# Two graph-attention layers, 16 batches: row sums of three groups counted in two parts, bias added by GpSimd, small transfers at other steps

## The chip, the cores and the metric

The kernel runs on one core of one Trainium2 chip. The metric is the device time of one execution in microseconds (us). The engines are called here as the profile calls them: PE (TensorE, matrix products; PEld is its weight load), DVE (VectorE), ACT (ScalarE), POOL (GpSimd) and SP (SyncE, which here only issues transfers).

## The reference

Sixteen graphs of 1024 nodes with 256 features go through two layers. Each is a layer norm, a relu, a masked multi-head attention and a residual sum. Layer 0 has 4 heads of 64, layer 1 has 8 heads of 32 and biases on its projections.

```python
# layer 0
h = relu(layernorm(x))
x = x + attention(h, adj > 0, heads=4) @ Wo0.T + bo0
# layer 1
h = relu(layernorm(x))
x = x + attention(h, adj != 0, heads=8) @ Wo1.T + bo1
# attention, per head:
scores = q @ k.T / sqrt(D)
scores = where(mask, scores, -inf)
out = softmax(scores) @ v
```

## The kernel before

Everything is float32. For one batch, one layer and one half of the 512 query columns (`qh` 0 or 1) there are two **groups** (`g` 0 or 1). A group holds 128 feature rows: four heads of layer 1, or two heads of layer 0. It walks over the keys in **steps**, `j` = 0 to 7 in layer 1 and 0 to 3 in layer 0. A step works on one tile `p` of 128 x 4 x 512 numbers:

- `scores` (L448): four products on PE into two PSUM pairs `ps`. The pool of such pairs, `ps_s`, has three buffers, and the projections and `py` take theirs from it as well.
- `exponentials`: for each of the two pairs, DVE applies the mask and writes to `p` (L464), then ACT takes the exponential in place (L470).
- `weigh` (L482), two steps later (`LEAD = 2`): `p` times the values, summed over the steps in `po`.

The softmax sum over the keys needs the sum of all eight `p` of a group. In **layer 1** `count_steps` makes it. After each odd step, POOL adds the odd tile to the even one (L583, 128 x 2048 numbers), which leaves four tiles: (0,1), (2,3), (4,5), (6,7). Transfers issued by POOL with an addition at the target (`accumulate`, L569, 1 MB each) join them: (2,3) += (0,1) after step 3; (4,5) += (2,3) when step 7 comes up; (6,7) += (4,5) three steps later. Each waits, on POOL's own queue, until the one before has landed. Then `count` (L344) sums over the partitions on PE by four products with a column of ones, and adds up over its calls in PSUM `pz`. Even tiles have seven buffers (`p0`), odd ones two (`p1`). So the DVE operation of an odd step can write only when POOL has added the odd tile of four steps before. In **layer 0** `add_tiles` sums with DVE (L491, L494) and POOL (L494, L495, L497), without transfers.

When a group ends, `end_group` puts `spread` (ACT copies the sums out, SP sends them), `invert` (DVE), `fetch` (SP), `normalize` (POOL, L400) and, for the second group of a half, `end_half` (L430, L435) at fixed distances `at` from the step at hand.

**Order.** The whole program is one list of steps; `Stream.later(i, f)` puts a piece of work behind the instructions of step `i`, and `Stream.run` emits them. Nothing is reordered afterwards: each engine and each queue follows that written order. The work between is therefore a timetable. One **round** is 48 steps: `a` is the step at which layer 0 of batch b+1 begins (16 steps, round steps 0 to 15), `c` = `a` + 16 that at which layer 1 of batch b begins (round steps 16 to 47, four groups of eight). "Step 44" below is round step 44, the fifth step of the last group. A step that is followed by a projection or `py` (a "large" one) puts off its `weigh` to the next step.

Within a round the timetable also places, for batches ahead: the mask's load by POOL (`load`, L145), its transposition by SP (`flip`, L151) and its move to fp8 by ACT (`put`, L160); the statistics of a layer norm on DVE (L188 to L197, with L202 and L204 on POOL), the norm on ACT (L213); the addition of the output bias to `x` (`add_bias`, L222, a transfer with addition that POOL issues); `turn_blocks` on DVE (L239), then `put_blocks` and `place_blocks` (L244, L251), by which SP sends the transposed blocks to DRAM and back. The tile `adj` that a mask load fills has one buffer, so a load waits on POOL's queue until the flip of the one before has landed.

`gr.last` marks the fourth group of a layer, `gr.brief` that of batch 14, `gr.pairs` all groups of batch 15's layer 1; these have ways of their own.

Of the kernel before, what the change touches and what calls it, by code (L numbers as in the profile page):

```python
# [15 lines left out]
ALU = mybir.AluOpType  # L16
PSUM = bass.MemoryType.PSUM

P = 128
# [66 lines left out]
def fast_program(ctx, tc, a, w, loads, chk):  # L86
# [3 lines left out]
    nc = tc.nc  # L90
    x, adj, out = a["x"], a["adj"], a["out"]
    B, N, E = x.shape
    NT = N // P
# [42 lines left out]
    class Mask:  # L136
        def __init__(self, b):
            self.b, self.src, self.flipped, self.m = b, {}, {}, {}
# [32 lines left out]
    class Inputs:  # L171
# [47 lines left out]
        def add_bias(self, half):  # L219

            rows = xs[self.b, half]
            nc.gpsimd.dma_start(  # L222
                rows, w.bo[self.layer].unsqueeze(1).to_broadcast([P, 4, E]), accum_op=ALU.add
            )

        def blocks(self, half):
# [88 lines left out]
    class Group:  # L315


        def __init__(self, inp, mask, qh, g, half):
            self.inp, self.mask, self.qh, self.g, self.half = inp, mask, qh, g, half
            self.layer = inp.layer  # L320
            self.D = E // HEADS[self.layer]
            self.per = P // self.D
            self.scale = 1.0 / math.sqrt(self.D)
            self.n = f"{inp.n}_{qh}_{g}"
            self.n_f = self.per * 512 // P
            self.last = qh == QH - 1 and g == 1

            self.hurry = False

            self.brief, self.pairs = self.last and inp.b == B - 2, False  # L330

# [176 lines left out]
    class Stream:  # L508
# [12 lines left out]
        def later(self, i, f, *args):  # L521
            self.due.setdefault(i, []).append((f, args))
# [48 lines left out]
        def count_steps(self, i, st):  # L571


            gr, j = st.gr, st.j
            if gr.hurry and j >= NT - 2:
                if st.last:
                    self.counted(i, gr)
                gr.count(st.p, False, st.last)
            elif j % 2:
                one = self.steps[i - LEAD - 1].p  # L580
                if not (gr.brief or gr.pairs) and j == 7:
                    self.accumulate(gr.two, gr.one)
                nc.gpsimd.tensor_add(one, one, st.p)  # L583
                if gr.pairs:
                    self.later(i + 2, gr.count, one, j == 1, st.last)
                elif j == 1:
                    gr.one = one
                elif j == 3:
                    self.accumulate(one, gr.one)
                    gr.one = one  # L590
                    if gr.brief:
                        self.later(i + 8, gr.count, one, True, False)
                elif gr.brief:
                    self.later(i + (6 if j == 5 else 4), gr.count, one, False, st.last)
                elif j == 5:
                    gr.two = one
                else:
                    self.later(i + (1 if gr.last else 3), self.accumulate, one, gr.two)
                    self.later(i + (4 if gr.last else 8), gr.count, one, True, True)

        def counted(self, i, gr):

# [4 lines left out]
        def end_group(self, i, gr):  # L607

            if gr.hurry:
                for f in (gr.spread, gr.finish, gr.inp.test):  # L610
                    self.later(i, f)
                return

            if gr.layer == 0:
                self.later(i + 4, gr.count_added)
                at = 4, 6, 7, 9, 11
            else:
                at = (8, 12, 14, 17, 19) if gr.qh == 0 else (8, 11, 12, 14)
                if gr.pairs:
                    at = 2, 5, 6, 7, 9  # L620
                elif gr.last:
                    at = 4, 6, 7, 9, 11
            for k, f in zip(at, (gr.spread, gr.invert, gr.fetch, gr.normalize)):
                self.later(i + k, f)
            if gr.last:

                k = 7 if gr.layer or gr.inp.b == 0 else 37
                self.later(i + k if gr.inp.b + gr.layer < B - 1 else len(self.steps) + 2, gr.inp.test)
            if gr.g == 1:
                self.later(i + at[4], gr.end_half)  # L630
# [8 lines left out]
    mask, inp = masks[0], inputs[0][0]  # L639
# [73 lines left out]
    stream = Stream(steps)  # L713
    later = stream.later

    def norms(inp, half, *at, whole=False):

        for i, f in zip(at, (inp.stats, inp.stats, inp.norm, inp.norm)):
            rest = (whole,) if i in at[2:] else ()
            later(i, f, half, (0, 1) if i in (at[0], at[2]) else (2, 3), *rest)  # L720
        later(at[3] + 1, inp.add_bias, half)

    def half_inputs(inp, half, *at):

        for i, f in zip(at, (inp.turn, inp.k, inp.q, inp.values)):
            later(i, f, half)

    def block_inputs(inp, half, turn, place, *at):

        later(turn, inp.turn_blocks, half)  # L730
        later(place, inp.put_blocks, half)
        later(place + 1, inp.place_blocks, half)
        for i, f in zip(at, (inp.k, inp.q, inp.values)):
            later(i, f, half)

# [4 lines left out]
    for t in range(NT):  # L740
        i = 5 + 2 * t
        later(i - 3, masks[1].load, t)
        later(i - 2, masks[1].flip, t)
        later(i, masks[1].put, t)
    later(9, bias_of_v)
    norms(inputs[0][1], 0, 2, 3, 5, 6, whole=True)
    half_inputs(inputs[0][1], 0, 7, 8, 10, 12)
    norms(inputs[0][1], 1, 6, 7, 9, 10, whole=True)
    half_inputs(inputs[0][1], 1, 13, 14, 20, 16)
    for b in range(B - 1):  # L750
        mine, a, c = inputs[1][b], first[b + 1], second[b]
        if b == 0:

            norms(mine, 0, a + 5, a + 6, a + 8, a + 9, whole=True)
            half_inputs(mine, 0, a + 11, a + 12, a + 14, a + 14)
            norms(mine, 1, a + 13, a + 14, a + 15, c, whole=True)
            half_inputs(mine, 1, c + 1, c + 3, c + 6, c + 4)
        else:
            norms(mine, 0, a - 20, a - 19, a - 16, a - 15)
            block_inputs(mine, 0, a - 14, a - 12, a, a + 2, a + 8)  # L760
            norms(mine, 1, a - 14, a - 10, a - 8, a - 6)
            block_inputs(mine, 1, a, a + 6, c, c + 6, c + 2)
        for i, u in zip((0, 2, 4, 6, 8, 10, 12, 13), range(NT)):
            later(a + i, masks[b].second, u)
        if b + 2 < B:
            other, mask = inputs[0][b + 2], masks[b + 2]
            later(a + 5, open_x, b + 2, 0)
            later(a + 13, open_x, b + 2, 1)
            if b == 0:
                norms(other, 0, a + 14, a + 15, c + 2, c + 3)  # L770
                block_inputs(other, 0, c + 4, c + 5, c + 8, c + 16, c + 18)
                norms(other, 1, c + 3, c + 4, c + 6, c + 7)
                block_inputs(other, 1, c + 10, c + 11, c + 22, c + 26, c + 30)
            else:
                norms(other, 0, a + 10, a + 12, a + 13, a + 15)
                block_inputs(other, 0, c, c + 1, c + 8, c + 16, c + 18)
                norms(other, 1, c, c + 4, c + 5, c + 6)
                block_inputs(other, 1, c + 7, c + 8, c + 22, c + 26, c + 30)
            for i, t in zip((7, 12, 17, 22, 33, 37, 41, 45), range(NT)):
                later(a + i - 5, mask.load, t)  # L780
                later(a + i - 3, mask.flip, t)
                later(a + i, mask.put, t)
        else:
            last, e = inputs[1][b + 1], c + 32
            norms(last, 0, c + 5, c + 6, c + 8, c + 9)
            block_inputs(last, 0, c + 10, c + 11, c + 14, c + 16, c + 20)
            norms(last, 1, c + 13, c + 14, c + 16, c + 17)
            block_inputs(last, 1, c + 18, c + 19, c + 24, e + 6, e + 4)
            for u in range(NT):
                later(c + 8 + 2 * u, masks[b + 1].second, u)  # L790
    stream.run()
# [157 lines left out]
def kernel(  # L949
# [28 lines left out]
    with ExitStack() as fast, tc.manual_schedule():  # L978
        fast_program(fast, tc, a, w, loads, chk)
# [61 lines left out]
```

## Time and profile before

| | us |
|---|---|
| median of 3 runs | 3362.56 (3353.72 to 3362.99) |
| the profiled execution | 3362.77 |
| its span, first to last instruction | 3360.8 |
| one round in the middle (batch 4: layer 0 of batch 5 and layer 1 of batch 4) | 207.6 |

| engine | busy us | what it mostly does |
|---|---|---|
| PE | 3221.9 (96%) | L448 1214.2, L482 1013.4, L344 148.6 |
| DVE | 2514.4 (75%) | L464 1795.6, 1.214 each |
| ACT | 2254.8 (67%) | L470 1614.8, 1.056 each |
| POOL | 2317.3 (69%) | L583 1195.1, 4.689 each |

Every product of the program stands in the trace as two matmul records, so a step has 8 records on L448 and 8 on L482, a count in layer 1 has 8 on L344. Instructions of PE and DVE follow each other in order. Busy PE time holds time at a lower clock as well: the profile gives the granted clock beside it. A `p<-p` transfer takes 9.3 us from its issue to its landing (median of 178; 7.0 to 23.5), an `x<-bo` transfer 5.9 (64), a mask load 4.3 (128).

### The profile page before, as it was taken

How to read it: one execution, taken by the hardware profiler on the slowest of the kernel's cores; microseconds unless marked ns; L12 is line 12 of the kernel's file. 1: busy time of each engine (PE TensorE's matmuls, PEld its weight loads, DVE VectorE, ACT ScalarE, POOL GpSimd, SP SyncE). 2: the span in 40 equal slices, each digit the busy share in tenths (PEclk: the TensorE clock that was granted, in tenths of full speed). 3: DMA queues.
4: the chain of work that ended last, by engine and by line, in shares of the span. 5: the costliest groups of instructions: out<-in, count | busy, mean ns of one | idle time of the engine just before them, and what ended most of it. 6: DMA issues, size and time to landing. Idle time of an engine off the chain costs nothing.

```text
span 3360.8 us, 44052 instructions
## 1 busy us (share of the span) xinstructions
PE 3221.9 (96%) x16302; PEld 1225.2 (36%) x16302; DVE 2514.4 (75%) x2786; ACT 2254.8 (67%) x2472; POOL 2317.3 (69%) x1146
## 2 busy tenths in 40 slices
PE   8999998999999999999999999999999999999998
PEld 3433433334334333333333334333343333433332
DVE  5677785877868778687786868768687786877766
ACT  5666676676767666676676676766766676776765
POOL 3567576676766758677586776767767686685776
PEclk9999998999999999999999999999999999999999
DMA  7347569495684857758477584866839568493441
GB/s 144 61 82 154 119 137 139 93 168 117 137 156 99 162 111 143 152 106 163 107 152 139 116 159 103 156 123 132 157 92 168 114 140 152 97 172 78 104 89 31
DMA packets 388063, 421.93 MB, mean 126 GB/s; under 512 B 197760, under 2 KB 324992, under 8 KB 365056
## 3 DMA queue, kind: packets, MB, share of 16 engines
q0 software_dynamic: 77856, 253.78, 42.7%
q1 hardware_dynamic: 309984, 165.26, 21.2%
q8 instruction: 130, 2.13, 0.3%
q14 instruction: 93, 0.76, 0.1%
HBM read 149.95 MB, written 47.96 MB: 59 GB/s over the span
## 4 chain that ended last, share of the span: by engine, by line
PE 84%; DMA 6%; POOL 4%; DVE 3%; issue 1%; ACT 1%; SPq 0%; POOLq 0%; DVEq 0%; ACTq 0%
PE ps L448 30%; PE po L482 25%; PE pq L269 12%; PE py L430 7%; PE pv L305 7%; POOL p L583 4%; DMA adjT<-adj 3%; PE pz L344 3%; DVE p L464 2%; DMA p<-p 1%; ACT p L470 0%; ACT mask L160 0%; DMA vd<-vn 0%; DMA hT<-turned 0%; POOL p L569 0%
## 5 line engine op out<-in xcount | busy, mean ns | idle before, releaser
L464 DVE SCALAR_TENSOR_TENSOR p<-mask,ps 128x1024 f32<-128x1024 fp8e5 x1536 | 1795.6, 1214 | 621.4 <-PE ps L448 506.2
L470 ACT ACTIVATE p<-p 128x1024 f32<-128x1024 f32 x1536 | 1614.8, 1056 | 879.6 <-DVE p L464 835.4
L583 POOL TENSOR_TENSOR p<-p,p 128x2048 f32<-128x2048 f32 x255 | 1195.1, 4689 | 201.5 <-PE po L482 190.7
L448 PE MATMUL ps<-qT,kT 32*128 32x512 f32 (+1 forms) x6144 | 1214.2, 649 | 92.6 <-DVE p L464 90.5
L482 PE MATMUL po<-p,v 128*32 128x512 f32 (+1 forms) x6144 | 1013.4, 617 | 1.8 <-ACT cat L355 1.6
L448 PEld LDWEIGHTS ps<-qT,kT 32*128 32x128 f32 (+1 forms) x6144 | 383.6, 188 | 848.1 <-issue 376.1
L495 POOL TENSOR_TENSOR p<-p 128x1024 f32<-128x1024 f32 x128 | 302.4, 2363 | 316.5 <-DVE p L494 307.7
L482 PEld LDWEIGHTS po<-p,v 128*32 128x32 f32 (+1 forms) x6144 | 229.9, 119 | 708.6 <-issue 481.2
L494 POOL TENSOR_TENSOR p<-p 128x1024 f32<-128x1024 f32 x64 | 151.0, 2359 | 230.8 <-DVE vn L384 146.0
L269 PE MATMUL pq<-hT,wk 128*128 128x512 f32 x512 | 244.3, 621 | 14.4 <-DMA hT<-turned 5.7
L569 POOL DMA_DIRECT2D p<-p x178 | 177.8, 999 | 104.9 <-DMA p<-p 70.2
L269 PE MATMUL pq<-hT,wq 128*128 128x512 f32 x512 | 239.6, 611 | 0.0
L305 PE MATMUL pv<-wv,hT 128*128 128x256 f32 x1024 | 237.8, 385 | 0.0
L430 PE MATMUL py<-wo,cat 128*128 128x256 f32 x1008 | 233.5, 385 | 1.4
L305 PEld LDWEIGHTS pv<-wv,hT 128*128 128x128 f32 x1024 | 189.4, 190 | 71.3 <-issue 22.7
L430 PEld LDWEIGHTS py<-wo,cat 128*128 128x128 f32 x1008 | 186.6, 190 | 70.6 <-issue 43.0
L400 POOL TENSOR_TENSOR cat<-cat,inv 128x512 f32<-128x512 f32 x127 | 173.5, 1366 | 7.1 <-DMA inv<-vd 3.7
L160 ACT ACTIVATE mask<-adjT,numbers 128x1024 fp8e5<-128x1024 bf16 x124 | 140.8, 1136 | 30.2 <-DMA adjT<-adj 30.2
L491 DVE TENSOR_TENSOR p<-p 128x1024 f32<-128x1024 f32 x128 | 158.9, 1241 | 0.0
L497 POOL TENSOR_TENSOR p<-p,p 128x1024 f32<-128x1024 f32 x64 | 151.9, 2373 | 5.0
L269 PEld LDWEIGHTS pq<-hT,wk 128*128 128x128 f32 x512 | 94.9, 195 | 159.9 <-issue 114.7
L355 ACT COPY cat<-po 128x512 f32<-128x512 f32 x128 | 74.0, 578 | 117.8 <-PE po L482 117.7
(51 smaller groups left out, 1689.1 us busy)
## 6 DMA issues: line engine op xcount, KB each, us to landing
p<-p POOLq DMA_DIRECT2D x178, 1024.0 KB, 9.3
adj<-in_adj_dram POOLq DMA_DIRECT2D x128, 256.0 KB, 4.3
x<-bo POOLq DMA_DIRECT2D x64, 512.0 KB, 5.9
turned<-hn SPq DMA_DIRECT2D x58, 512.0 KB, 2.9
hT<-turned SPq DMA_DIRECT2D x232, 128.0 KB, 5.2
x<-in_x_dram SPq DMA_DIRECT2D x128, 128.0 KB, 2.7
inv<-vd SPq DMA_DIRECT2D x128, 128.0 KB, 3.0
inv<-vd SPq DMA_DIRECT2D x252, 64.0 KB, 3.1
```

Source lines behind the costliest of these rows:

```text
L269: nc.tensor.matmul(pq[:, m, :], wt[self.layer][:, c, ts(m, P)], self.hT[half][:, c, :], start=(c == 0), stop=(c == 1),)
L305: nc.tensor.matmul(pv[:, i, :], self.hT[half][:, c, ts(i, P)], w.v[self.layer][:, c, :], start=(c == 0), stop=(c == 1),)
L400: nc.gpsimd.tensor_mul(o, o, self.inv)
L430: nc.tensor.matmul(py[:, i, :], self.half.cat[:, c, ts(i, P)], w.o[self.layer][:, c, :], start=(c == 0), stop=(c == 1),)
L448: nc.tensor.matmul(st.ps[i // 2][:, i % 2, :], gr.inp.kT[r * D : (r + 1) * D, gr.g, ts(kt, P)], gr.inp.qT[gr.qh][r * D : (r + 1) * D, gr.g ...
L464: nc.vector.scalar_tensor_tensor(out=half, in0=gr.mask.m[gr.qh][:, kt, :].unsqueeze(1).to_broadcast([P, 2, 512]), scalar=-EDGE if gr.layer ...
L470: nc.scalar.activation(half, half, AF.Exp, scale=gr.scale)
L482: nc.tensor.matmul(gr.o[r * D : (r + 1) * D, :], gr.inp.v[:, kt, h * D : (h + 1) * D], st.p[:, i, :], start=(kt == 0), stop=(kt == NT - 1),)
L491: nc.vector.tensor_add(a, a, b)
L495: nc.gpsimd.tensor_add(a, a, b)
L569: nc.gpsimd.dma_start(one, two, accum_op=ALU.add)
L583: nc.gpsimd.tensor_add(one, one, st.p)
```

## The change

Groups of layer 1 that are not the last of their layer (nor batch 15's) no longer join (2,3) to (4,5). The tile with (0..3) is counted by itself, `wait` steps after its transfer was issued; (6,7) += (4,5) is issued as soon as POOL has made (6,7), and the tile is counted `wait` steps later into the same PSUM. `add_bias` becomes a sum by POOL, and some of these sums, the steps of the mask's loads, flips and puts, of `place_blocks`, and of `spread`, `invert`, `fetch` and `normalize` are moved.

```diff
         def add_bias(self, half):
             rows = xs[self.b, half]
-            nc.gpsimd.dma_start(
-                rows, w.bo[self.layer].unsqueeze(1).to_broadcast([P, 4, E]), accum_op=ALU.add
+            nc.gpsimd.tensor_add(
+                rows, rows, w.bo[self.layer].unsqueeze(1).to_broadcast([P, 4, E])
             )
...
+            self.wait = 8 if qh or g else 6
...
-                if not (gr.brief or gr.pairs) and j == 7:
+                if gr.last and not (gr.brief or gr.pairs) and j == 7:
                     self.accumulate(gr.two, gr.one)
                 nc.gpsimd.tensor_add(one, one, st.p)
...
                 elif j == 3:
                     self.accumulate(one, gr.one)
                     gr.one = one
+                    if not gr.last:
+                        self.later(i + gr.wait, gr.count, one, True, False)
...
                 elif j == 5:
                     gr.two = one
+                elif not gr.last:
+                    self.accumulate(one, gr.two)
+                    self.later(i + gr.wait, gr.count, one, False, True)
                 else:
-                    self.later(i + (1 if gr.last else 3), self.accumulate, one, gr.two)
-                    self.later(i + (4 if gr.last else 8), gr.count, one, True, True)
+                    self.later(i + 1, self.accumulate, one, gr.two)
+                    self.later(i + 4, gr.count, one, True, True)
...
-                at = (8, 12, 14, 17, 19) if gr.qh == 0 else (8, 11, 12, 14)
+                at = (8, 11, 15, 17, 19) if gr.qh == 0 else (8, 11, 13, 15)
+                if gr.wait == 6:
+                    at = 6, 11, 15, 17
...
-    def norms(inp, half, *at, whole=False):
+    def norms(inp, half, *at, whole=False, bias=None):
...
-        later(at[3] + 1, inp.add_bias, half)
+        later(at[3] + 1 if bias is None else bias, inp.add_bias, half)
...
-    def block_inputs(inp, half, turn, place, *at):
+    def block_inputs(inp, half, turn, put, place, *at):
         later(turn, inp.turn_blocks, half)
-        later(place, inp.put_blocks, half)
-        later(place + 1, inp.place_blocks, half)
+        later(put, inp.put_blocks, half)
+        later(place, inp.place_blocks, half)
...
-            norms(mine, 0, a - 20, a - 19, a - 16, a - 15)
-            block_inputs(mine, 0, a - 14, a - 12, a, a + 2, a + 8)
-            norms(mine, 1, a - 14, a - 10, a - 8, a - 6)
-            block_inputs(mine, 1, a, a + 6, c, c + 6, c + 2)
+            norms(mine, 0, a - 20, a - 19, a - 16, a - 15, bias=a)
+            block_inputs(mine, 0, a - 14, a - 12, a - 8, a, a + 2, a + 8)
+            norms(mine, 1, a - 14, a - 10, a - 8, a - 6, bias=a + 6)
+            block_inputs(mine, 1, a, a + 6, a + 7, c, c + 6, c + 2)
...
                 norms(other, 0, a + 10, a + 12, a + 13, a + 15)
-                block_inputs(other, 0, c, c + 1, c + 8, c + 16, c + 18)
-                norms(other, 1, c, c + 4, c + 5, c + 6)
-                block_inputs(other, 1, c + 7, c + 8, c + 22, c + 26, c + 30)
-            for i, t in zip((7, 12, 17, 22, 33, 37, 41, 45), range(NT)):
+                block_inputs(other, 0, c, c + 1, c + 2, c + 8, c + 16, c + 18)
+                norms(other, 1, c, c + 4, c + 5, c + 6, bias=c + 42)
+                block_inputs(other, 1, c + 7, c + 8, c + 12, c + 22, c + 26, c + 30)
+            for i, t in zip((9, 13, 17, 22, 35, 39, 43, 47), range(NT)):
                 later(a + i - 5, mask.load, t)
                 later(a + i - 3, mask.flip, t)
                 later(a + i, mask.put, t)
```

The first round (b = 0) and the last inputs get the same three-place form of `block_inputs`, with the places one to four steps apart.

In round steps: a count falls on steps 33, 41, 1 and 5 before; on 27, 31, 37, 41, 45, 1 and 5 after. The bias stands at steps 34 and 43 (input of layer 1, halves 0 and 1) and 16 and 23 (input of layer 0) before, and at 0, 6, 16 and 10 after, the first two and the last then in layer 0 of the round that follows. Mask loads stand at 2, 7, 12, 17, 28, 32, 36 and 40 before, and at 4, 8, 12, 17, 30, 34, 38 and 42 after.

More of the change, by code (lines that the diff above doesn't have):

```diff
@@ L770, in fast_program @@
                 norms(other, 0, a + 14, a + 15, c + 2, c + 3)
-                block_inputs(other, 0, c + 4, c + 5, c + 8, c + 16, c + 18)
+                block_inputs(other, 0, c + 4, c + 5, c + 6, c + 8, c + 16, c + 18)
                 norms(other, 1, c + 3, c + 4, c + 6, c + 7)
-                block_inputs(other, 1, c + 10, c + 11, c + 22, c + 26, c + 30)
+                block_inputs(other, 1, c + 10, c + 12, c + 16, c + 22, c + 26, c + 30)
             else:
                 norms(other, 0, a + 10, a + 12, a + 13, a + 15)
-                block_inputs(other, 0, c, c + 1, c + 8, c + 16, c + 18)
-                norms(other, 1, c, c + 4, c + 5, c + 6)
-                block_inputs(other, 1, c + 7, c + 8, c + 22, c + 26, c + 30)
-            for i, t in zip((7, 12, 17, 22, 33, 37, 41, 45), range(NT)):
+                block_inputs(other, 0, c, c + 1, c + 2, c + 8, c + 16, c + 18)
+                norms(other, 1, c, c + 4, c + 5, c + 6, bias=c + 42)
+                block_inputs(other, 1, c + 7, c + 8, c + 12, c + 22, c + 26, c + 30)
+            for i, t in zip((9, 13, 17, 22, 35, 39, 43, 47), range(NT)):
                 later(a + i - 5, mask.load, t)
@@ L785, in fast_program @@
             norms(last, 0, c + 5, c + 6, c + 8, c + 9)
-            block_inputs(last, 0, c + 10, c + 11, c + 14, c + 16, c + 20)
+            block_inputs(last, 0, c + 10, c + 11, c + 12, c + 14, c + 16, c + 20)
             norms(last, 1, c + 13, c + 14, c + 16, c + 17)
-            block_inputs(last, 1, c + 18, c + 19, c + 24, e + 6, e + 4)
+            block_inputs(last, 1, c + 18, c + 19, c + 20, c + 24, e + 6, e + 4)
             for u in range(NT):
```

## The prediction

> **What bounds the kernel now.** First the page's shares and costliest lines, to see which engine leads.
>
> ```profile
> PE 3221.9 (96%) x16302; PEld 1225.2 (36%) x16302; DVE 2514.4 (75%) x2786; ACT 2254.8 (67%) x2472; POOL 2317.3 (69%) x1146
> L464 DVE SCALAR_TENSOR_TENSOR p<-mask,ps 128x1024 f32<-128x1024 fp8e5 x1536 | 1795.6, 1214 | 621.4 <-PE ps L448 506.2
> L448 PE MATMUL ps<-qT,kT 32*128 32x512 f32 (+1 forms) x6144 | 1214.2, 649 | 92.6 <-DVE p L464 90.5
> ```
>
> PE seems to be the bound, and its idle time (3360.8 - 3221.9 = 139 us) small. But 90.5 us of it are waits of a score product for L464, and busy time may hide a low clock. So next the same work is compared in two places of one round (batch 4). Steps 34 to 39 and 42 to 47 have the same shape (large pair, small pair, large pair) and the same 124 matmul records; their bounds are the first score products in PE's timeline.
>
> ```profile
> core 0: us, PE busy (x) PEld busy (x) DVE busy (x) ACT busy (x) POOL busy (x), PEclk, DMA share, GB/s
> 1124.75:1145.28 20.53, 20.53 (x124) 7.99 (x120) 17.07 (x24) 17.09 (x20) 17.55 (x10) 1.00 0.75 145
> 1150.64:1178.70 28.06, 23.85 (x124) 8.44 (x121) 15.66 (x15) 17.71 (x21) 20.01 (x10) 0.88 0.79 150
> ```
>
> The second stretch is 28.06 - 20.53 = 7.5 us longer: 4.2 idle, and 23.85 - 20.53 = 3.3 "busy" at a granted clock of 0.88. PE's and POOL's timelines say why.
>
> ```profile
> 1158.32 1.13 PE L448 MATMUL ps<-qT,kT 32*128 32x512 f32 x4
> 1163.65 2.08 PE L448 MATMUL ps<-qT,kT 32*128 32x512 f32 x4 [4.21 <-DVE p L464]
> ```
>
> ```profile
> 1142.61 0.86 POOL L569 DMA_DIRECT2D p<-p  x1 [0.30 <-POOL p L583]
> ...
> 1144.76 4.56 POOL L583 TENSOR_TENSOR p<-p,p 128x2048 f32<-128x2048 f32 x1
> 1153.88 0.64 POOL L145 DMA_DIRECT2D adj<-in_adj_dram  x1 [4.55 <-DMA adjT<-adj]
> 1156.93 0.88 POOL L569 DMA_DIRECT2D p<-p  x1 [2.42 <-PE ps L448]
> 1157.51 4.83 POOL L583 TENSOR_TENSOR p<-p,p 128x2048 f32<-128x2048 f32 x1
> ```
>
> ```profile
> 1142.61 13.78 DMA p<-p
> ```
>
> Between 1149.3 and 1157.5 POOL adds nothing. It waits for the flip (L145), then for the transfer of 1142.61, which takes 13.78 us in the chain of waits and lands at 1156.38; the releaser named for L569 only came last. Behind it stands the addition of step 41, which frees the odd buffer that step 43's L464 needs: DVE waits 5.65 us for that L583, then PE 4.21 for DVE. This occurs in each of rounds 0 to 13, with PE gaps of 3.0 to 4.3 us, and 13.86 in round 1. A second gap, 2.0 us per round, stands at step 31:
>
> ```profile
> 1107.70 2.02 DVE L192 SCALAR_TENSOR_TENSOR ve<-mv 128x4 f32<-128x4 f32 x1
> ```
>
> L192 takes 0.16 us at its least and here ends with POOL's L583 (1105.16 + 4.54 = 1109.70).
>
> **What the change takes away.** *The join on POOL's queue.* The second transfer, which waits for the first, is gone in 15 batches x 3 groups = 45 of 178 transfers; the last one follows its own addition and waits for nothing else. Step 41's addition can start at 1149.4 instead of 1157.5, and step 43 finds its buffer at about 1154, when its scores are there (1155.39 + 1.1). Gain up to 7.5 us in 14 rounds = 105. In round 1 step 44 lasts 18.85 us against 9.21 in round 4, so 9.6 more. **Gross: 114.6.** If the cover fails the waits stand as now, and the gain is nil; that is a rival.
>
> *Bias transfers.* Three of a round's four leave layer 1's POOL queue (1.35 to 1.66 us each). POOL is late there only behind the wait just counted, so no further gain.
>
> **What it adds.** *Counts:* 45 more, of 8 matmul records. Step 33 has a count and lasts 1124.75 - 1120.97 = 3.78; step 35 is the same without one, 1132.40 - 1129.47 = 2.93. So 0.85 each, 38.3 in all. Three per round are not equal: that at 27 falls where DVE has no idle time (L464 follows L464 from 1096.72 to 1101.33) and PE waits for pairs, so I count 0.2, minus 9 over 14 rounds. That which moves from 33 to 31 comes behind the 2.0 us gap, where L448 records take 1.02 instead of 0.59 us: up to 0.85 more a round, plus 6 taken for half of them. **35.** Bounds: 15 (all but those at 45 hidden, 15 x 0.85 + 2) and 50 (none hidden, all low clocks paid).
>
> *Landings that PE now waits for.* First counts come 6 or 8 steps after the issue. By the least steps (2.07 and 2.93) 6 are over 15 us; the median landing is 9.3. The tightest is group 0's second count, issued at about 1097, due after 1112. Nil; at 13.8 as at step 39 still nil, at the longest, 23.5, 8 us once.
>
> *Moved small transfers.* The mask load of step 40 stood ahead of step 41's addition; now that of 42 stands ahead of step 43's. It still waits for a flip, two steps before, as before. Step 43's addition can't start before its `weigh`, 1157.5. The flip of 38 was issued at 1142.1 and landed at 1153.3, 11.2 us, beside two large transfers; from step 40 (about 1147) that gives 1158. `normalize` (L400, 1.3 us) waits for `fetch` in the same place. Behind them is step 43's addition, which frees step 45's L464 (due 1161.5, buffer ready at 1158 + 0.6 + 4.6 = 1163). I take 1.5 us lost per round, **21**; bounds 0 and 5, which is the loss of now less what is gone: 0 to 70. ACT's `put` moves with its flip and stands before a large pair's slack at 47; nil, at 1.1 us per round otherwise. The hT transfers, three steps later, have ten steps to their use: nil.
>
> *Bias on POOL.* The nearest row is L494 on POOL, 128x1024, 2.36 us; four per round, all at steps 0 to 16. There PE is the bound (60.0 of 60 us busy from 1200 to 1260) and POOL 34.4 of 60. At 0 it fills a wait (3.07 us before the transfer at 1185.72), at 16 it fits ahead of DVE's next sum. At 6 and 10 it meets DVE: L291, L491 and POOL hold each other up, as L192 shows (0.16 to 2.02). A sum held for 2.2 us at 6, with DVE's own slack at steps 7 and 8 of 0.2 and 0.1, reaches PE through the pairs, less the one pair of lead (1.2). I take 0.7 per round, **10**; bounds 0 and 4.7 (two sums, nothing hidden): 0 to 66.
>
> A rule speaks against this part. The Trainium skill, "SBUF — State Buffer", section "SBUF: two separate sides": GpSimd and a DVE operation with two SBUF inputs lock one port pair for a whole instruction, and the loser stops. The L192 row agrees. By the rule alone each of about 60 sums could stop DVE for all of its length, an estimate of 60 x 2.36 = 142 us, which would make the change slower; by the rows only two of four stand where DVE has such an operation.
>
> A second rule concerns the gain. "TensorE: Matmul & The Clock Gate", section "What's actually happening": an idle window of about 3.4 us halves PE's clock until it has been busy for one. The trace lowers it sooner: the 2.0 us gap at step 31 leaves 0.77 over 1104 to 1118, the 4.2 us one 0.88 over its stretch; idle time alone would give 4.2 x 14 = 59 instead of 105, so removing a gap should return more than the gap.
>
> **Sum.** 3362.8 (the profiled execution; median 3362.6, so nothing to correct) - 114.6 + 35 + 21 + 10 = **3314**. Step 31's gap stays, since its L583 waits for PE (1.29 us idle before it), not for a transfer.
>
> **Rivals.**
> *More goes than I allow:* landings are quicker with fewer transfers, nothing replaces the wait, DVE is never held: 3362.8 - 114.6 + 35 = 3283, less with counts hidden (15): 3263. For it: the DMA share of 1.01 at 1140 to 1158. Against: POOL is busy 17.55 of 20.53 us even undisturbed.
> *The wait moves:* the mask load, 4.55 us of the wait of now, holds up step 43's addition and PE loses 5 to 5.5 at step 45. 3362.8 - 114.6 + 35 + 77 + 10 = 3370; with the lower count price 3350. For it: flips of 8 to 11 us. Against: that addition has to wait for PE until 1157.5 anyway.
> *Slower, by the port:* the sums at 6 and 10 stop DVE in each round where it has no slack, and the clock falls as at step 31. From 3.5 us lost per round (49 / 14) this decides; at 4.7, and 1.0 for the clock, 15 x 5.7 = 86 in place of 10: 3390. For it: L291 of 2.30 and L192 of 2.02 us. Against: PE has no gap at all in layer 0, at the same locks.
> *It doesn't do what it says:* POOL would still wait ahead of its additions. The written order leaves only the flip, so that is the second rival.
>
> **How the numbers follow.** My case (3285 to 3345) 0.53, more 0.20, the wait moves 0.15, the port 0.12. A change under about 0.3% (10 us) can't be told from none: 3352.5 to 3372.6. Faster: 0.53 + 0.20 + 0.02 of the moved wait = 0.75; same: 0.08 of it and 0.01 of the port = 0.09; slower: 0.05 + 0.11 = 0.16. The range 3270 to 3378 leaves out about a tenth on each side.
>
> **What would show it.** POOL without an idle stretch ahead of the additions of steps 41 and 43; steps 42 to 47 at 21 to 24 us instead of 28.06, at full clock; 45 x 8 = 360 more records on L344; 133 `p<-p` transfers; L222 at 2.36 us in POOL's rows; layer 0 still at 80 us a round, and L491 not above 1.3 us on average. I am wrong if a gap of 3 us or more stands at step 45, if layer 0 grows by over 2 us, or if counts wait for landings.

## The result, and the profile after

| | us |
|---|---|
| the changed kernel, median of 4 | 3397.94 (3396.04 to 3404.77) |
| the kernel before, same comparison, median of 4 | 3358.14 (3353.49 to 3362.99) |
| ratio | 1.0122, 95% interval 1.0098 to 1.0146 |

The change makes the kernel 1.2% slower, where 3314 and a gain had been forecast. The page of the changed kernel (from L330 on, the changed kernel's lines stand two further down than in the kernel before: L346 is the count, L386 invert, L388, L378 and L396 the transfers around it, L402 normalize, L466 the masking of the exponentials, L571 the joining transfer, L585 the addition):

```profile
PE 3235.6 (95%) x16662; PEld 1243.8 (37%) x16662; DVE 2561.6 (75%) x2786; ACT 2245.8 (66%) x2472; POOL 2353.2 (69%) x1101
L222 POOL TENSOR_TENSOR x<-x,bo 128x1024 f32<-128x1024 f32 x64 | 151.7, 2371 | 17.2 <-DMA bo<-in_bo_dram 17.2
p<-p POOLq DMA_DIRECT2D x133, 1024.0 KB, 7.7
adj<-in_adj_dram POOLq DMA_DIRECT2D x128, 256.0 KB, 6.3
```

The parts are there: 360 more matmul records (16302 to 16662), 133 joining transfers, the sum of the bias at 2.371 us on POOL. In the median the joining transfers have become quicker (9.3 to 7.7 us) and the mask loads slower (4.3 to 6.3). That last line is the first sign.

Where the time went is seen by the lengths of the 48 steps of a round, each taken from its first score product to the next step's. Below are means over rounds 4 to 12, in which nearly every step has the same length in each round; steps 31 and 32 vary with the clock, and step 46 of the changed kernel goes from 10.1 to 17.4 us. Only these steps differ by more than 0.02 us:

| round step | 12 | 27 | 28 | 31 | 32 | 33 | 37 | 38 | 42 | 44 | 45 | 46 | round |
|---|---|---|---|---|---|---|---|---|---|---|---|---|---|
| before | 5.57 | 2.35 | 5.61 | 5.96 | 5.61 | 3.78 | 2.44 | 5.46 | 5.25 | 8.30 | 3.23 | 5.09 | 205.70 |
| changed | 5.69 | 3.21 | 4.75 | 7.29 | 5.02 | 2.92 | 3.30 | 4.70 | 4.73 | 2.07 | 3.30 | 15.40 | 209.44 |

The stall at step 44 is gone (-6.23), and a larger one stands at step 46 (+10.31). The same comparison of equal stretches as before the change, steps 34 to 39 and 42 to 47 of round 4, each with 133 matmul records, and layer 0 (steps 0 to 15) in the third row:

```profile
core 0: us, PE busy (x) PEld busy (x) DVE busy (x) ACT busy (x) POOL busy (x), PEclk, DMA share, GB/s
1130.61:1151.25 20.64, 20.64 (x133) 7.97 (x129) 17.89 (x25) 16.56 (x19) 17.80 (x10) 1.00 0.69 141
1156.61:1187.99 31.38, 25.30 (x133) 10.29 (x129) 15.72 (x15) 16.76 (x20) 16.28 (x8) 0.84 0.61 126
980.08:1060.06 79.98, 79.98 (x349) 31.25 (x345) 64.65 (x65) 52.58 (x58) 54.26 (x28) 1.00 0.43 93
```

The loss over the undisturbed stretch is 31.38 - 20.64 = 10.7 us, where it was 7.5 before. Layer 0 takes 79.98 us against 79.86: the sums on POOL cost PE 0.12 us there. POOL's and DVE's timelines of the stall:

```profile
1150.63 9.10 POOL L585 TENSOR_TENSOR p<-p,p 128x2048 f32<-128x2048 f32 x2 [0.65 <-issue]
1160.02 0.91 POOL L571 DMA_DIRECT2D p<-p  x1 [0.30 <-POOL p L585]
1160.66 0.85 POOL L145 DMA_DIRECT2D adj<-in_adj_dram  x1
1169.79 1.26 POOL L402 TENSOR_TENSOR cat<-cat,inv 128x512 f32<-128x512 f32 x1 [8.28 <-DMA inv<-vd]
1171.01 8.97 POOL L585 TENSOR_TENSOR p<-p,p 128x2048 f32<-128x2048 f32 x2
```

```profile
1171.22 0.25 DVE L386 RECIPROCAL vn<-sums 128x16 f32<-128x16 f32 x1 [3.45 <-DMA sums<-s]
1175.53 4.62 DVE L466 SCALAR_TENSOR_TENSOR p<-mask,ps 128x1024 f32<-128x1024 fp8e5 x4 [4.06 <-POOL p L585]
```

The additions of steps 39 and 41 (9.10 us for two) now follow each other without a pause, as the change wants it. Then POOL stands still for 8.28 us: `normalize` of group 0 (L402), written for step 42, waits for `inv`, and the additions of steps 43 and 45 are queued behind it. DVE stops twice, first in `invert` of group 1 (L386), which waits for the sums that SP sends, then for POOL's addition. In the waits between engines the two have these rows (total, times, longest):

```profile
POOL cat L402 <- DMA inv<-vd: 126.6, 15, 11.2
```

```profile
DVE vn L386 <- DMA sums<-s: 61.5, 14, 5.9
```

For the kernel before the first row is 3.7 us, once:

```profile
POOL cat L400 <- DMA inv<-vd: 3.7, 1, 3.7
```

It has no row like the second. SP's queue tells why `inv` and the sums are late (start, time in issue, what):

```profile
1146.13 0.38 SPq L388 DMA_DIRECT2D vd<-vn  x1
1156.33 1.24 SPq L151 DMA_TRANSPOSE adjT<-adj  x1
1157.67 2.59 SPq L251 DMA_DIRECT2D hT<-turned  x4
1160.36 2.99 SPq L396 DMA_DIRECT2D inv<-vd  x4
1163.46 4.02 SPq L378 DMA_DIRECT2D sums<-s  x4
```

From 1146.5 to 1156.3 SP waits to send one flip, that of step 40. It needs the mask load that POOL issued at 1147.79, right after the joining transfer of 1147.03, and that load lands only at 1156.27, 8.5 us later. `place_blocks`, `fetch` and `spread` follow in order. The first two stand there by the change: before, `place_blocks` stood at step 37 and this `fetch` at 39, behind the flip of step 38. So the `inv` transfers go out from 1160.36 on, beside the next joining transfer (1160.02): the first lands at 1163.80, the other three at 1168.5 to 1169.6. In the kernel before, none of the 128 mask loads is issued within 1.5 us after a joining transfer; in the changed one 36 are, and their median time to landing is 8.9 us, that of the others 4.6 (both counted from issues and landings in the trace).

### The profile page after: what moved, and what is told of

Read it like the earlier page. It is cut to its first block, busy times and chain, and to the rows that moved or that the text cites. A ratio compares the mean times of both kernels' runs of the same rounds, so it can differ in the third digit from the quotient of the medians.

```text
span 3402.6 us, 44513 instructions
## 1 busy us (share of the span) xinstructions
PE 3235.6 (95%) x16662; PEld 1243.8 (37%) x16662; DVE 2561.6 (75%) x2786; ACT 2245.8 (66%) x2472; POOL 2353.2 (69%) x1101
## 4 chain that ended last, share of the span: by engine, by line
PE 87%; DMA 3%; SPq 2%; POOL 2%; DVE 2%; issue 1%; ACT 1%; POOLq 0%; DVEq 0%; ACTq 0%
PE ps L450 30%; PE po L484 26%; PE pq L269 12%; PE pv L305 8%; PE py L432 7%; PE pz L346 5%; DMA inv<-vd 3%; POOL p L585 2%; DVE p L466 2%; SPq L251 1%; SPq L396 1%; ACT p L472 1%; DMA hT<-turned 0%; ACT mask L160 0%; ACT hn L213 0%
## 5 line engine op out<-in xcount | busy, mean ns | idle before, releaser
L466 DVE SCALAR_TENSOR_TENSOR p<-mask,ps 128x1024 f32<-128x1024 fp8e5 x1536 | 1797.1, 1213 | 563.4 <-PE ps L450 476.6
L585 POOL TENSOR_TENSOR p<-p,p 128x2048 f32<-128x2048 f32 x255 | 1163.9, 4574 | 333.3 <-issue 178.3
L450 PE MATMUL ps<-qT,kT 32*128 32x512 f32 (+1 forms) x6144 | 1176.3, 640 | 128.2 <-DVE p L466 126.4
L484 PE MATMUL po<-p,v 128*32 128x512 f32 (+1 forms) x6144 | 995.3, 604 | 2.1 <-ACT cat L357 1.8
L450 PEld LDWEIGHTS ps<-qT,kT 32*128 32x128 f32 (+1 forms) x6144 | 373.0, 187 | 851.9 <-issue 350.8
L402 POOL TENSOR_TENSOR cat<-cat,inv 128x512 f32<-128x512 f32 x127 | 185.1, 1458 | 130.6 <-DMA inv<-vd 126.6
L305 PE MATMUL pv<-wv,hT 128*128 128x256 f32 x1024 | 265.2, 417 | 0.0
L305 PEld LDWEIGHTS pv<-wv,hT 128*128 128x128 f32 x1024 | 209.1, 209 | 88.0 <-DVE p L466 43.3
L346 PE MATMUL pz<-p,ones 128*32 128x512 f32 (+1 forms) x1248 | 204.6, 624 | 0.8 <-ACT s L365 0.8
L222 POOL TENSOR_TENSOR x<-x,bo 128x1024 f32<-128x1024 f32 x64 | 151.7, 2371 | 17.2 <-DMA bo<-in_bo_dram 17.2
L168 ACT ACTIVATE mask<-mask,numbers 128x1024 fp8e5<-128x1024 fp8e5 x128 | 145.0, 1133 | 0.0
```

The source lines that it names most:

```text
L305: nc.tensor.matmul(pv[:, i, :], self.hT[half][:, c, ts(i, P)], w.v[self.layer][:, c, :], start=(c == 0), stop=(c == 1),)
L346: nc.tensor.matmul(self.s[r * self.D : (r + 1) * self.D, :], w.ones.to_broadcast([P, self.D]), p[:, r, :], start=start, stop=stop,)
L402: nc.gpsimd.tensor_mul(o, o, self.inv)
L450: nc.tensor.matmul(st.ps[i // 2][:, i % 2, :], gr.inp.kT[r * D : (r + 1) * D, gr.g, ts(kt, P)], gr.inp.qT[gr.qh][r * D : (r + 1) * D, gr.g ...
L466: nc.vector.scalar_tensor_tensor(out=half, in0=gr.mask.m[gr.qh][:, kt, :].unsqueeze(1).to_broadcast([P, 2, 512]), scalar=-EDGE if gr.layer ...
L484: nc.tensor.matmul(gr.o[r * D : (r + 1) * D, :], gr.inp.v[:, kt, h * D : (h + 1) * D], st.p[:, i, :], start=(kt == 0), stop=(kt == NT - 1),)
```

## The experiments

Theory F was that the joins and counts do what was forecast, and that the whole loss is a wait for small transfers: first for `fetch` (F), later, when half of the loss had stayed, for `fetch` and for the sums (F2). Against it stood W, that the counts and sums are too much work; D, that large transfers make every fetch slow wherever it stands; and the port, that POOL's sums stop DVE. All times are medians of 4 runs or more, with the ratio to the kernel before and its 95% interval.

**One wait away, in two ways.** Normalize later, behind the additions (`e1`), or the fetch ahead of the flip (`e2`), at step 39, where it stood before the change:

```diff
                 if gr.wait == 6:
-                    at = 6, 11, 15, 17
+                    at = 6, 11, 15, 21      # e1: normalize at step 46 instead of 42
+                    at = 6, 11, 14, 17      # e2: fetch at step 39 instead of 40
```

> The changed kernel with one number changed: normalize of the first group of layer 1 stands at round step 46 instead of 42, behind the additions of steps 43 and 45 on POOL's queue. Theory F (a wait for the fetch): the changed kernel loses 10.3 us a round at step 46 because normalize, waiting 8.3 us for inv, holds up those additions; then step 46 falls from 15.4 to 5 to 6 us and the time to 3398 - 14 x 10 = 3258, between 3245 and 3280. Rival W (work): the 45 counts on PE and 64 sums on POOL are simply too much there, inv only comes last; then the additions are late anyway and the time stays above 3375.

> The changed kernel with fetch of the first group at round step 39 instead of 40, so that SP sends it ahead of the flip of step 40; normalize stays at 42. Theory F with SP's order as the cause (the flip waits 9 us for a mask load, the fetch stands behind it and then goes out beside the next accumulation): inv lands before 1157 on round 4's clock, normalize waits less than 1 us, 3245 to 3285. If instead the accumulations make any fetch slow wherever it stands (rival D), inv lands late all the same, normalize waits 3 us or more and the time stays above 3310. Rival W: above 3375.

Measured: 3328.8 us (0.9897, 0.9857 to 0.9938) and 3324.6 (0.9885, 0.9842 to 0.9927). Both missed their numbers: too good for W, and only half of what F had said. The wait for `inv` is down to 3.9 us in the whole span when the fetch leaves one step earlier, so D is out for it, and the place of `fetch` behind the late flip is its cause. But step 46 still takes 11.13 and 10.44 us. The waits of DVE in the run with the fetch early:

```profile
DVE vn L386 <- DMA sums<-s: 60.1, 17, 5.3
```

This wait, 60.1 us against 61.5, had been covered by the other. The instruction that waits is `invert` of group 1, which the change moved from step 45 to 44 (12 to 11 steps after the group's end). The sums it waits for land later, too: in round 4 the last of them 19.9 us after the start of step 40 (1171.10 - 1151.25), before the change 15.9 (1161.14 - 1145.28). No run separates the two; the run that follows moves `invert` alone.

**Invert alone, and both.** `invert` of group 1 at step 46 with normalize left at 42 (`e10`), and with normalize at 46 as well (`e7`):

```diff
-                at = (8, 11, 15, 17, 19) if gr.qh == 0 else (8, 11, 13, 15)
+                at = (8, 13, 15, 17, 19) if gr.qh == 0 else (8, 11, 13, 15)
```

> The changed kernel with invert of group 1 at step 46 instead of 44 and normalize left at 42. Theory F2 (two waits that cover each other): the addition held up by normalize still frees the buffer only at the same moment, so little or nothing is gained, 3380 to 3400; the gain of both (138 us) is then more than the sum of one alone (69) and the other (under 20). If the waits add up instead, invert alone gives the other half, 3320 to 3340.

> The changed kernel with two numbers changed: normalize of group 0 at step 46 instead of 42 (as in the run with normalize late) and invert of group 1 at step 46 instead of 44. Theory F2 (two waits stand one behind the other: normalize on POOL for inv, invert on DVE for the sums, 4.3 us): with both away step 46 falls from 15.4 to 5 to 6 us and the time to 3398 - 14 x 10 = 3258, between 3245 and 3275. Rival: late small transfers find a third place to hold something up (the masks' put on ACT, end_half's product on PE), 3290 or more. Rival W (work): stays at 3325, as with one wait away.

Measured: invert alone 3400.6 us (1.0126, 1.0097 to 1.0156), both 3259.5 (0.9692, 0.9666 to 0.9718). Against the changed kernel's 3397.9, normalize late alone gives 69, invert late alone nothing, both 138. Step 46 is at 15.19 with invert alone and at 4.72 with both, which is an undisturbed large step (4.70 at 38). Two waits that overlap behave so: as long as the later one stands, nothing is gained by removing the earlier, and removing the later one alone gives back only what it adds to the earlier, here half.

**The mask's steps.** The changed kernel with loads, flips and puts where they were before:

```diff
-            for i, t in zip((9, 13, 17, 22, 35, 39, 43, 47), range(NT)):
+            for i, t in zip((7, 12, 17, 22, 33, 37, 41, 45), range(NT)):
```

> The changed kernel with the mask's loads, flips and puts at the steps of the kernel before (loads 28, 32, 36, 40). Theory F: the load of 36 leaves ahead of the transfer of step 37 and lands in 4 to 5 us, the flip of 38 doesn't wait, the fetch of 40 goes out before the accumulation of step 41: normalize waits 0 to 3 us, 3250 to 3310. Rival D: the wait for inv stays near 8 us and the time above 3375. Rival W: above 3375.

Measured: 3272.6 us (0.9726, 0.9689 to 0.9763). This undoes one line of the change, two steps of distance, and turns 1.2% slower into 2.7% faster. Mask loads land in 4.2 us again:

```profile
adj<-in_adj_dram POOLq DMA_DIRECT2D x128, 256.0 KB, 4.2
```

None of them is issued within 1.5 us after a joining transfer. Step 46 takes 7.08 us, with 32.0 us of waits for the sums left in `invert`.

**The counts alone.** The kernel before with the counting in two parts and the new `at`, without the bias on POOL, the mask's and `place_blocks`' new steps:

> The kernel before with the counting in two parts and the new steps of spread, invert, fetch and normalize, nothing else: bias by transfer, mask and place at their old steps. Theory F: the wait for the join is gone and the fetch of 40 follows a flip of 38 whose load left early; POOL still issues the bias at steps 34 and 43; 3270 to 3320. Rival W with the counts as the cost: 45 counts at 0.85 us above the kernel before less nothing, 3375 to 3400.

Measured: 3294.9 us (0.9800, 0.9764 to 0.9837). The counting by itself gains 2%. W falls.

**All but the counts.** The other way round, with the counting and the `at` of before:

> The changed kernel with the counting of before (three joining transfers, one count, old steps of spread, invert, fetch and normalize); bias on POOL and the new steps of mask and place stay. Theory F2: mask loads two steps later leave behind a joining transfer and land late, and the join on POOL's queue is back, so it is no faster than the kernel before: 3350 to 3400. If moving the mask and the bias is what the gain hangs on, and the counting only costs (rival W): 3300 to 3345.

Measured: 3378.3 us (1.0038, 1.0018 to 1.0058), with step 46 at 14.18. The new timetable is thus harmful without the counts too. Its waits on POOL:

```profile
POOL adj L145 <- DMA adjT<-adj: 104.3, 30, 6.2
POOL p L571 <- DMA p<-p: 55.0, 31, 3.5
```

Here POOL waits for the join and for the flip in front of the additions, as in the kernel before. But the flip now holds up the addition of step 43 instead of that of 41, and the stall stands at step 46 instead of 44 (2.34). 14 loads are issued within 1.5 us after a joining transfer; they take 10.7 us.

**The bias.** The changed kernel with the bias by a transfer again, at the new steps:

```diff
-            nc.gpsimd.tensor_add(
-                rows, rows, w.bo[self.layer].unsqueeze(1).to_broadcast([P, 4, E])
+            nc.gpsimd.dma_start(
+                rows, w.bo[self.layer].unsqueeze(1).to_broadcast([P, 4, E]), accum_op=ALU.add
             )
```

> The changed kernel with the bias added by a transfer again, at the new steps. Theory F2: in layer 0 the sum on POOL costs PE 0.1 us a round, so nothing changes: 3385 to 3405. Rival (the port): the sums stop DVE, and without them the time falls by 20 us or more, below 3378.

Measured: 3406.3 us (1.0125, 1.0094 to 1.0156), just above the expected band and not to be told from the changed kernel. Layer 0's step 12 goes back from 5.69 to 5.57 us, and that is all that the sums cost PE here. They do hold DVE up: L291 is busy for 87.1 us in the changed kernel and for 54.9 us without them.

**The gap at step 31.** The kernel before with one number changed:

```diff
-            norms(mine, 0, a - 20, a - 19, a - 16, a - 15)
+            norms(mine, 0, a - 20, a - 18, a - 16, a - 15)
```

> The kernel before with one number changed: the second statistics call of layer 1's input, half 0, at step 30 instead of 29. Theory (the port): L192 then starts after the addition of step 29 has ended and takes 0.2 instead of 2.0 us; the gap of 2.0 us at step 31 goes and with it the low clock; steps 31 and 32 take 3 us a round less, 3362 - 14 x 3 to 4 = 3305 to 3325. Rival: steps 28 to 31 are bound by DVE's work in any case, the gap stays in another place: above 3345.

Measured: 3324.3 us (0.9895, 0.9867 to 0.9924). Steps 31 and 32 of round 4 with the same 37 matmul records, first before, then with the number changed (columns as above):

```profile
1107.83:1120.97 13.14, 11.12 (x37) 3.18 (x33) 8.83 (x8) 7.32 (x8) 9.95 (x7) 0.74 0.98 174
```

```profile
1093.00:1101.91 8.91, 8.33 (x37) 2.79 (x33) 7.35 (x12) 6.68 (x7) 8.54 (x6) 1.00 1.06 212
```

PE's idle time fell from 2.02 to 0.58 us, and 4.2 us came back: the other 2.8 are the clock, 0.74 before. But round 4 is one of the two worst for the clock. The gap at step 31 is 2.0 us in each of rounds 4 to 12; in two of them the clock stays at 1.00, as in round 7 of the kernel before (columns as above):

```profile
1726.92:1737.09 10.17, 8.15 (x37) 2.71 (x33) 8.74 (x8) 6.68 (x7) 9.10 (x6) 1.00 0.99 187
```

In five rounds it is 0.85 (11.48 to 11.54 us), in two 0.74 (13.13 and 13.14). The mean return is 11.57 - 8.91 = 2.7 us a round, 1.3 of it the gap (10.17 - 8.91) and the rest the clock. The Trainium skill, "TensorE: Matmul & The Clock Gate", section "HAM oscillation — how this bites in real kernels", gives the rule as no idle gaps of PE over about 3.4 us. By this measurement 2.0 us is too long already in seven rounds of nine.

**The version that beats both.** Both waits away, the mask at its old steps, and the statistics one step later (the edits of `e7`, `e3` and `e9` on the changed kernel):

> The kernel of the run before with the mask at its old steps and one statistics call of layer 1's input moved from step 29 to 30, so that L192 comes after the addition of step 29 and not under it. Theory F2 and the port at step 31: the round loses 2.0 us of gap and about 2 of low clock at steps 31 and 32 besides; 3272 - 14 x (2 + 4) = 3190, between 3180 and 3215. If L192 then meets the next addition instead, 3240 to 3260.

Measured: 3199.9 us (0.9514, 0.9488 to 0.9539), 4.9% faster than the kernel before.

```profile
PE 3160.2 (99%) x16662; PEld 1217.1 (38%) x16662; DVE 2535.2 (79%) x2786; ACT 2247.2 (70%) x2472; POOL 2356.2 (74%) x1101
```

PE is busy for 99% of the span at a mean granted clock of 0.997, and rounds 1 to 13 take between 195.2 and 195.6 us each. PE's busy time is lower than in either kernel (3221.9 and 3235.6), though it does the counts: part of what was called busy had been a low clock.

The runs in one table, as means of rounds 4 to 12:

| kernel | 28 | 31 + 32 | 44 | 46 | round | median |
|---|---|---|---|---|---|---|
| before | 5.61 | 11.57 | 8.30 | 5.09 | 205.70 | 3358.1 |
| changed | 4.75 | 12.31 | 2.07 | 15.40 | 209.44 | 3397.9 |
| normalize late (e1) | 4.74 | 11.79 | 2.07 | 11.13 | 204.71 | 3328.8 |
| fetch early (e2) | 4.75 | 12.18 | 2.07 | 10.44 | 204.40 | 3324.6 |
| invert late (e10) | 4.74 | 11.64 | 2.07 | 15.19 | 208.56 | 3400.6 |
| both late (e7) | 4.74 | 12.93 | 2.07 | 4.72 | 199.38 | 3259.5 |
| mask's old steps (e3) | 4.75 | 11.69 | 2.07 | 7.08 | 200.50 | 3272.6 |
| counts alone (e5) | 4.75 | 11.86 | 3.19 | 7.17 | 201.54 | 3294.9 |
| no counts (e4) | 5.75 | 10.62 | 2.34 | 14.18 | 207.37 | 3378.3 |
| bias by transfer (e6) | 4.74 | 12.34 | 2.07 | 16.07 | 210.02 | 3406.3 |
| before, one number (e9) | 5.68 | 8.91 | 7.93 | 5.18 | 203.32 | 3324.3 |
| best (e8) | 4.74 | 8.91 | 2.07 | 4.72 | 195.35 | 3199.9 |

## Why the prediction was wrong

**The reading of what bounds the kernel** was right. Step 44's stall came from the flip and the join on POOL's queue; it is gone (8.30 to 2.07 us), and over all rounds step 44 alone gives back 97.8 of the 114.6 us forecast. The counts alone, with the loads at their old steps, bring it to 3.19; the loads moved without the counts only carry it over to step 46.

**The counts** were sized too high: 35 us, or 2.5 a round. Steps 27 and 28 together stay as they were (7.96 and 7.96 us), so do 37 and 38 (7.90 and 8.00), and 31 to 33 even lose 0.1. There PE waited for DVE and filled the wait. Only the count at 45 costs its 0.85 or so, about 12 us in all: step 45 was slowed by the clock before (3.23 us, where step 37 of the same form took 2.44) and takes 3.30 with the count. This is just below the lower bound of 15 that the prediction gave.

**The bias on POOL** was sized at 10 us, 0.7 a round. It costs 0.12 a round at step 12. The port does hold DVE up (L291, 54.9 to 87.1 us), but hardly any of it reaches PE. The rival built on it is refuted by the run with the bias as a transfer.

**The landings that PE waits for** cost nothing, as said; no row of waits names one.

**"Moved small transfers" is the step that failed.** It took 1.5 us lost per round, with 5 as the upper bound; the measured loss is 10.3. The place was nearly right (`normalize` behind `fetch` was named, and the flip), the size not, for three reasons:
- `normalize` was taken to wait for `fetch` "in the same place". But the change had moved `fetch` from step 39 to 40 and `place_blocks` from 37 to 40, to behind the flip of step 40. In round 4 the fetch goes out 9.1 us after the start of step 40 instead of 3.3, and beside the next joining transfer. Back at step 39 (`e2`) it costs nothing.
- SP's queue was not walked. The landing of the flip had been allowed for: at 1158, which is 12.7 us after the start of step 40, where it came after 8.15 (1159.40 - 1151.25). But it was sent late rather than slow: its load stands directly behind a joining transfer in POOL's queue and takes 8.5 us, SP holds the flip back for it, and all that stands behind the flip waits with it. With the loads at their old steps (`e3`) the wait for `inv` is 4.7 us in the whole span. The landings behind the flip were taken one by one, as if each went out at its step.
- `invert` of group 1, moved one step forward, does not occur in the sum. It is an instruction of DVE that waits for a transfer of SP, with all of DVE's further work behind it. Moved later alone it gains nothing; with the other wait away it is worth 69 us.

The upper bound of 5 us was "the loss of now less what is gone". A wait that moves is not bounded by the one it replaces: what is late next depends on which queue it stands in. In place of 21 us the term is 14 x 10.3 = 144 us. With it, and with the counts at 12 and the bias at 2, the prediction's own sum gives 3362.8 - 114.6 + 12 + 144 + 2 = 3406, where the runs gave 3396.0 to 3404.8.

**The rivals.** "The wait moves" is what happened, at 0.15, with another carrier (`normalize` and `invert` instead of the mask load before step 43's addition) and at step 46 instead of 45, with twice the price. The gap at step 31 stayed, as forecast.

## What to carry to other kernels

When work is moved in a kernel whose order is written out, follow each queue, not each transfer: for every moved issue list what it now stands behind on its own queue, and what waits behind it, down to the instruction of a busy engine that waits for the last of them. Issue small loads ahead of a large transfer on a queue, not after it, and put instructions that wait for a transfer as late as their consumers allow. When a stall stays after its cause has been removed, look for a second wait under it before giving up the theory: here one of two gave 69 us alone, the other nothing, and both together 138.

## What the runs showed of the hardware

- A 256 KB mask load lands in a median of 4.6 us, and in 8.9 us when it is issued within 1.5 us after a 1 MB transfer on the same queue (36 against 92 loads of the changed kernel). The Trainium skill, "DMA: Bandwidth & Descriptors", section "Queues, rings and completion order", says where it treats the queues of SP and ACT that descriptors of one queue are consumed in order on each DMA engine. These transfers are of POOL's queue; each of the 36 loads lands after the large transfer ahead of it, which fits such an order. No run separates the order from the mere load of the DMA engines.
- The same page says there that a DMA engine takes turns between queues, packet by packet. That does not make small transfers of another queue safe: the 64 or 128 KB `inv` transfers that SP issues within 4 us after a 1 MB one take 7.6 us in the median (47 in the changed kernel), the others 2.6. It does not always happen: with the mask at its old steps the 18 such ones took 2.3.
- A PE gap of 2.0 us lowered the granted clock of the stretch around it in seven of nine rounds (0.85 or 0.74 over 11.5 or 13.1 us) and left it at 1.00 in two. On average the gap and its clock cost 2.7 us a round; a gap of 0.58 us in the same place lowered the clock in none of the nine.
